# Transfers of the attention sums, their place in a written order, and a smaller piece for an accumulating DMA

## The chip, the cores and the metric

The kernel runs on one core of one Trainium2 chip. A core has five engines: TensorE (PE; its weight loads are listed as PEld), VectorE (DVE), ScalarE (ACT), GpSimd (POOL) and SyncE (SP), which here only issues DMAs. Sixteen DMA engines move the data. The metric is the device time of one execution in microseconds; the median of three runs before the change is 3682.39 us.

## The reference

A batch of 32 sequences of 256 tokens with 256 features goes through two layers. The first layer, cut to what matters here:

```
x  = x + attn(cond(x))                    # cond: modulated linear, attention over the 16 heads
                                          # of one token, modulated linear
                                          # attn: 16 heads of 16, normed queries and keys, gated
h  = adapter(x, cond_512)                 # per-sequence weights: x W_down relu W_up + x
x  = x + h-block:  h1 = h + self_attention(layer_norm(h))
                   moe(layer_norm(h1))    # 8 experts, top 2, capacity a quarter of the tokens
```

The second layer (a modulated linear map, an elementwise attention, a conditioned network, a butterfly FFN) follows. A softmax attention is computed for each head as exp(scores) times values, divided by the sum of the exp's; these divisors are the "sums" below.

## The kernel before, in words

The program has two phases. The first one runs, for each of the 32 sequences, everything up to the expert router (`sequence`); the second runs the experts and the second layer. Each phase's steps are written as Python generators. A step says `yield ENGINE, cost` ahead of the instructions that it issues, `yield None, t` for a time in which it only waits, `yield DMA, t` for a time on the shared transfer path, and takes and gives back buffers or turns (`Turns(n)`: n may be inside at a time). `side_by_side` reads these costs, keeps a clock for each engine, and always lets the step go on that can start first, where a step's `rank` breaks ties; the rank is the sequence's number plus the entry of its stage in the table `STAGES`. The result is one fixed order of instructions on every engine, made when the program is built. The costs are no times of the chip: they only decide the order. On the chip every engine runs its own list in order and waits at the head of it when an operand is not there. SP's DMAs and POOL's DMAs are such lists too. At most nine sequences are under way (`lanes`).

What the change touches, by name and line:

- `head_softmax_attention` (from L765): the attention over heads of a token. For sequences 3 to 31, `summed` adds two products of 128 x 2048 floats into one by a DMA with `accum_op=add` that POOL issues (L848, on buffers `hprod` of the ring `hp`, which has 5); then DVE halves the rest three times (L854, L856) and scales (L858). There are two such DMAs for each of these 29 sequences.
- `attention` (from L1033), run twice for each sequence. Scores (L1081), exp (L1090), answers (L1063), copied to `avT` (L1070). Of every 32 rows of `avT`, the first 16 hold answers and row 16 a sum. Behind the stage `tokens`: a DMA brings the sums into `den` as 128 x 32 (L1109); DVE takes reciprocals (L1118, into `den` or `sums`); a DMA stores them to `rden` in HBM (L1120); four DMAs move half of the answers up beside the others (L1124); a DMA reads `rden` back, each row repeated for 16 features, into `oT` (L1128); DVE multiplies (L1135).
- `residual_in`: loads `x` (L1188); POOL adds a bias row (L1190). `adapter_weights`: loads two rows to all partitions (L1172, L1174); POOL makes `wd` (L1177, L1178) and `wu` (L1181, L1182), which have two buffers each. TensorE uses them at L1306 and L1323.
- `layer_norm`: DVE's statistics (L366, L367), POOL's power (L261, L267, called `rstd`), DVE's scaling (L289, `xh`). The norms of queries take POOL's power at the same lines (called `n`), and DVE uses them at L918. The same POOL list holds L848, L1190, and these.

The DMAs of the first phase are issued by SP, except for L848 and one early load.

Of the kernel before, what the change touches and what calls it, by code (L numbers as in the profile page):

```python
# [14 lines left out]
F = mybir.dt.float32  # L15
I32 = mybir.dt.int32
AF = mybir.ActivationFunctionType
ALU = mybir.AluOpType
# [4 lines left out]
P = 128  # L23
S = 256
D = 256
H = 16
DH = 16
# [7 lines left out]
PE, DVE, ACT, POOL, SP = "PE", "DVE", "ACT", "POOL", "SP"  # L35
DMA = "DMA"
DVE2 = "DVE2"
POW = "POW"
# [61 lines left out]
def side_by_side(parts, lags):  # L100
# [84 lines left out]


STAGES = {
    "in": -0.5,
    "heads": 30.0,
    "answers of heads": 6.5,  # L190
    "sums of heads": -6.5,
    "out of heads": -25.0,
    "queries": 11.5,
    "queries by token": -7.5,
    "scores 1": -15.0,
    "tokens 1": 20.5,
    "out 1": 0.5,
    "x1": -12.0,
    "adapter": -13.0,
    "norm 1": -12.5,  # L200
    "queries 2": 26.0,
    "scores 2": -29.0,
    "tokens 2": 4.0,
    "out 2": -0.5,
    "norm 2": -5.5,
    "gates": -19.0,
    "values": 8.5,
    "norms of queries": -6.0,
    "answers": 8.0,
    "tokens": 8.0,  # L210
    "residual in": -4.5,
    "adapter's weights": 21.5,
    "bias": 24.5,
    "residual out": 16.0,
}


# [1 line left out]
def network(ctx: ExitStack, tc: tile.TileContext, a: dict, out: bass.AP):  # L219
    nc = tc.nc  # L220
    T = out.shape[0]
    B = T // S
# [8 lines left out]
    dpool = ctx.enter_context(tc.tile_pool(name="dpool", bufs=1, space=DRAM))  # L231
# [4 lines left out]
    rbuf = rrows[:T, :].rearrange("(b p t) d -> b p (t d)", p=P, t=2)  # L236
    gbuf = dpool.tile([2 * T, 1], F, name="gbuf")
    DS = 2 * H
    rden = dpool.tile([2, B, P, DS], F, name="rden")
    gtab = dpool.tile([B, 2 * HID + 2 * D], F, name="gtab")  # L240

    ident = cst.tile([P, P], F, name="ident")
# [92 lines left out]
    def back(r):  # L335
        return "back", rings[r][2]
# [22 lines left out]
    def layer_norm(sm, x2, name):  # L359

        yield DVE, lengths["moments"]
        st = sm.tile([P, 2, 6], F, name="st")
        mv = sm.tile([P, 2, 2], F, name="mv")
        rstd = sm.tile([P, 2], F, name="rstd")
        for t in range(2):
            nc.vector.bn_stats(st[:, t, :], x2[:, t, :])  # L366
            nc.vector.bn_aggr(mv[:, t, :], st[:, t, :])  # L367
        yield lengths["power"], 1.25
        rsqrt(rstd, mv[:, :, 1], 2, LN_EPS)
        xh = yield from get("sh", name)  # L370
        yield DVE, 0.75
        normalize(xh, x2, mv, rstd)
        return xh
# [364 lines left out]
    sums = {}  # L738
# [26 lines left out]
    def head_softmax_attention(kk, o0, b, exact):  # L765
# [78 lines left out]
        def summed(t, one, two):  # L844

            yield "stage", "sums of heads"
            yield POOL, 1.3
            nc.gpsimd.dma_start(one, two, accum_op=ALU.add)  # L848
            yield DMA, 7.0
            yield None, 2.0  # L850
            yield back("hp")
            for n in (4, 2):
                yield DVE2, 0.1 + 0.27 * n
                nc.vector.tensor_tensor(one[:, :n], one[:, :n], one[:, n : 2 * n], ALU.add)  # L854
            yield DVE2, 0.8
            nc.vector.tensor_tensor(o0[:, t, :], one[:, 0], one[:, 1], ALU.add)  # L856
            o = o0[:, t, :].rearrange("p (h d) -> p h d", h=H)
            nc.vector.tensor_tensor(o, o, rs[:, t].unsqueeze(2).to_broadcast([P, H, DH]), ALU.mult)  # L858
            yield back("hp")
# [173 lines left out]
    def attention(l, hT, b, exact, beside=None):  # L1033


        va = vaug[l]
        qT = yield from get("qk", "qT")
        kT = yield from get("kT", "kT", TS)
        vals = Part(values(l, hT))
        if l == 1:  # L1040
            yield vals
            yield from cosine_queries_and_keys(hT, qT, kT)
        else:
            yield from plain_queries_and_keys(hT, qT, kT)
            yield vals
        if beside is not None:
            yield "join", beside
        yield "join", vals
        yield back("sh")
        nm = None  # L1050
        if exact and l == 2:
            both = yield from get("hp", "both")
            nm = yield from row_maxima(qT, kT, both)
        yield "stage", f"scores {l}"

        avT = yield from get("avT", "avT")

        def answers(c, pt, av):
            yield "stage", "answers"
            yield PEC, 0.9  # L1060
            for kc in range(2):
                for i in range(4):
                    nc.tensor.matmul(  # L1063
                        av[32 * i : 32 * i + 32, c % 2, :], va[:, kc, HO * (4 * c + i) : HO * (4 * c + i) + 32], pt[:, i, kc, :],
                        start=(kc == 0), stop=(kc == 1),
                    )
            yield back("pt")
            if c % 2 == 1:
                yield ACT, 0.6
                nc.scalar.copy(avT[:, c - 1 : c + 1, :], av)  # L1070
                yield back("av")

        last = None
        for c in range(4):
            m, e = c // 2, c % 2
            sc = yield from get("sc", "sc")
            yield PER, 0.98
            for kc in range(2):
                for i in range(4):
                    r = slice(32 * i, 32 * i + 32)  # L1080
                    nc.tensor.matmul(  # L1081
                        sc[:, i, kc, :], kT[r, m, kc * P : (kc + 1) * P], qT[r, e, m, :], start=True,
                        stop=nm is None,
                    )
                    if nm is not None:
                        r = slice(32 * i, 32 * i + 1)
                        nc.tensor.matmul(sc[:, i, kc, :], ones[r, :], nm[r, c, :], start=False, stop=True)
            pt = yield from get("pt", "pt")
            yield EXP, 1.88
            nc.scalar.activation(pt, sc, AF.Exp, scale=1.0 / math.sqrt(DH))  # L1090
            yield back("sc")
            if last is not None:
                yield "join", last
            if c % 2 == 0:
                av = yield from get("av", "av")
            last = Part(answers(c, pt, av))
            yield last
        if nm is not None:
            yield back("hp")
        yield back("qk")  # L1100
        yield back("kT")
        yield "join", last
        yield "back", vaug_turn[l]
        yield "stage", f"tokens {l}"

        den = yield from get("den", "den")
        lanes_of = avT.rearrange("(i s d) c x -> i s d (c x)", i=4, s=2)
        yield SP, 0.6
        nc.sync.dma_start(  # L1109
            den[:, 0, :], lanes_of[:, 1, 0].rearrange("i (k x) -> i k x", x=DS)  # L1110
        )
        yield None, 2.8
        rd = den[:, 1, :]
        if l == 2 and not exact:
            rd = sums[b // NR][:, 1, 2 * (b % NR) : 2 * (b % NR) + 2, :].rearrange("p t h -> p (t h)")
        oT = yield from get("sh", "oT", TS)
        yield DVE, 0.37
        nc.vector.reciprocal(rd, den[:, 0, :])  # L1118
        yield SP, 1.0
        nc.sync.dma_start(rden[l - 1, b], rd)  # L1120
        for i in range(4):
            r = 32 * i + DH
            yield SP, 0.6
            nc.sync.dma_start(avT[r : r + DH, :2, :], avT[r - DH : r, 2:, :])  # L1124
        yield None, 0.4
        yield back("den")
        yield SP, 0.6
        nc.sync.dma_start(  # L1128
            oT.rearrange("p c s -> p (c s)"),
            rden[l - 1, b].rearrange("(g k) x -> g (k x)", g=8).unsqueeze(1).to_broadcast([8, DH, 2 * S]),  # L1130
        )
        yield DMA, 1.5
        yield None, 2.3
        yield DVE2, 0.75
        nc.vector.tensor_tensor(oT, avT[:, :2, :], oT, ALU.mult)  # L1135
        yield back("avT")
        return oT
# [28 lines left out]
    def adapter_weights(b, wd, wu):  # L1166
# [5 lines left out]
        nc.sync.dma_start(g1, gtab[b : b + 1, : 2 * HID].to_broadcast([P, 2 * HID]))  # L1172
        yield SP, 1.0
        nc.sync.dma_start(g2, gtab[b : b + 1, 2 * HID :].to_broadcast([P, 2 * D]))  # L1174
        yield None, 2.5
        yield POOL, 1.6
        nc.gpsimd.tensor_tensor(wd, wdn, g1[:, :HID].unsqueeze(1).to_broadcast([P, 2, HID]), ALU.mult)  # L1177
        nc.gpsimd.tensor_tensor(wd, wd, g1[:, HID:].unsqueeze(1).to_broadcast([P, 2, HID]), ALU.add)  # L1178
# [6 lines left out]
    def residual_in(b, x):  # L1185
        yield "stage", "residual in"
        yield SP, 1.0
        nc.sync.dma_start(x, a["x"][b * S : (b + 1) * S, :].rearrange("(t p) d -> p t d", p=P))  # L1188
        yield POOL, 1.3
        nc.gpsimd.tensor_tensor(x, x, rowA("bo1").unsqueeze(1).to_broadcast([P, 2, D]), ALU.add)  # L1190

# [14 lines left out]

    lanes = Turns(9)
    pair_turn = Turns(1)

    def sequence(b, exact):  # L1210

# [60 lines left out]
        x = yield from get("sh", "x")  # L1272
        res = Part(residual_in(b, x))
        yield res
        wd = sm.tile([P, 2, HID], F, name="wd", bufs=2)
        wu = sm.tile([P, D], F, name="wu", bufs=2)
        wts = Part(adapter_weights(b, wd, wu))
# [43 lines left out]
        for t in range(2):  # L1321
            r = slice(t * HID, (t + 1) * HID)
            nc.tensor.matmul(ps[t], act[r, :], wu[r, :], start=True, stop=True)  # L1323
        yield back("sh")
        yield DVE, 0.85
        for t in range(2):
            nc.vector.tensor_add(c2[:, t, :], ps[t], x1[:, t, :])
# [1204 lines left out]
```

## Time and profile before

| | us |
|---|---|
| three runs | 3684.66, 3678.87, 3682.39; median 3682.39 |
| the profiled execution | 3687.47 |
| its span, from the first to the last instruction | 3685.7 |
| TensorE busy | 3461.0 (94%) |
| VectorE busy | 2256.0 (61%) |
| GpSimd busy | 1914.8 (52%) |
| ScalarE busy | 1791.0 (49%) |
| mean granted TensorE clock | 0.976 |

Busy time is that of instructions; waiting at the head of a list and issuing DMAs from SP is not in it. A wait is put down to what came last by the profile. TensorE's matmuls overlap and their ends are modelled, so its busy share is an upper bound of work.

### The profile page before, as it was taken

The numbers are of one execution on the slowest core, as the hardware profiler recorded it, in microseconds if no ns is written. First come the engines' busy times: TensorE is split into PE (matmuls) and PEld (weight loads), VectorE is DVE, ScalarE is ACT, GpSimd is POOL, SyncE is SP. The second block draws the span as 40 slices with busy tenths as digits, with TensorE's granted clock in tenths as the row PEclk, the third lists the DMA queues.
The fourth block names the chain that finished last, engine by engine and source line by source line (L and its number), as shares of the span: only waits on it lengthen the run. The fifth ranks groups of instructions, "written<-read, shape, count | busy, mean of one in ns | idle before, by whom it ended". The sixth has DMA issues, their size and how long they took to land. (4 is left out here: it accounts for less than half of the span.)

```text
span 3685.7 us, 54807 instructions
## 1 busy us (share of the span) xinstructions
PE 3461.0 (94%) x21429; PEld 2525.1 (69%) x21429; DVE 2256.0 (61%) x3608; ACT 1791.0 (49%) x2761; POOL 1914.8 (52%) x1571
## 2 busy tenths in 40 slices
PE   6898999899999999959999999999979999999999
PEld 5565666566666665636666666666968888888888
DVE  7897889888888884566664531101355656555554
ACT  2786777777777777732222222222223343333433
POOL 2666655554455654335546565553044656565553
PEclk9999999999999999979999999999989999999999
DMA  1333444443444442143334343332341323232331
GB/s 65 74 84 92 100 91 96 97 95 92 95 97 94 96 97 68 52 144 86 79 96 100 91 92 55 58 67 46 126 143 55 114 92 97 95 107 92 117 95 43
DMA packets 179406, 329.51 MB, mean 89 GB/s; under 512 B 42465, under 2 KB 104097, under 8 KB 169154
## 3 DMA queue, kind: packets, MB, share of 16 engines
q0 software_dynamic: 56480, 161.59, 19.8%
q1 hardware_dynamic: 122514, 163.79, 14.1%
q8 instruction: 172, 2.82, 0.3%
q14 instruction: 96, 0.79, 0.1%
q10 hardware_dynamic: 144, 0.52, 0.0%
HBM read 204.03 MB, written 51.53 MB: 69 GB/s over the span
## 5 line engine op out<-in xcount | busy, mean ns | idle before, releaser
L1090 ACT ACTIVATE pt<-sc 128x2048 f32<-128x2048 f32 x256 | 480.8, 1878 | 113.8 <-PE sc L1081 104.7
L1702 ACT ACTIVATE hid<-bh,cols 128x512 f32<-128x512 f32 x254 | 173.8, 687 | 620.5 <-PE bh L1713 602.0
L1728 PE MATMUL by<-w,hid 128*128 128x256 f32 x2048 | 454.1, 380 | 2.5 <-DVE ysb L1734 2.5
L1713 PE MATMUL bh<-ehT,w 128*128 128x512 f32 x1024 | 451.1, 594 | 1.1 <-DVE ysb L1734 1.1
L1728 PEld LDWEIGHTS by<-w,hid 128*128 128x128 f32 x2048 | 387.9, 191 | 68.3 <-issue 15.3
L267 POOL TENSOR_TENSOR n<-n,negh 128x32 f32<-128x32 f32 x64 | 362.8, 5669 | 5.3
L1636 POOL DMA_INDIRECT rrows<-ysb,row x128 | 216.0, 1687 | 251.6 <-DMA rrows<-ysb,row 142.0
L1713 PEld LDWEIGHTS bh<-ehT,w 128*128 128x128 f32 x1024 | 194.8, 191 | 221.0 <-issue 214.9
L1734 DVE TENSOR_TENSOR ysb<-by,b 128x512 f32<-128x512 f32 x64 | 44.0, 688 | 471.4 <-PE by L1728 384.5
L1081 PE MATMUL sc<-qT,kT 32*128 32x256 f32 x4096 | 297.7, 405 | 22.3 <-ACT pt L1090 22.0
L1063 PE MATMUL av<-pt,vaug 128*32 128x256 f32 x4096 | 279.9, 392 | 8.0 <-ACT pt L1090 7.8
L1081 PEld LDWEIGHTS sc<-qT,kT 32*128 32x128 f32 x4096 | 187.4, 186 | 120.9 <-issue 52.9
L893 DVE TENSOR_TENSOR hprod<-hex,kk 128x2048 f32<-128x2048 f32 x116 | 264.8, 2305 | 0.0
L2359 PE MATMUL dh<-zT,w_eff 128*128 128x256 f32 x1024 | 235.3, 379 | 0.0
L1669 POOL DMA_INDIRECT xg<-h2buf,tok x128 | 148.8, 1163 | 161.4 <-issue 54.3
L2373 PE MATMUL do<-w_con,gT 128*128 128x256 f32 x1024 | 230.9, 379 | 0.0
L2373 PEld LDWEIGHTS do<-w_con,gT 128*128 128x128 f32 x1024 | 192.3, 190 | 24.9
L261 POOL TENSOR_SCALAR rstd<-mv 128x2 f32<-128x2 f32 x160 | 61.7, 386 | 281.3 <-DVE mv L367 271.2
L2359 PEld LDWEIGHTS dh<-zT,w_eff 128*128 128x128 f32 x1024 | 189.9, 190 | 23.6 <-DVE zT L2335 0.3
L1063 PEld LDWEIGHTS av<-pt,vaug 128*32 128x32 f32 x4096 | 108.1, 110 | 133.6 <-issue 64.3
L848 POOL DMA_DIRECT2D hprod<-hprod x58 | 53.3, 924 | 252.7 <-DVE hprod L893 208.7
L793 DVE TENSOR_TENSOR hprod<-kk 128x2048 f32<-128x2048 f32 (+1 forms) x96 | 162.6, 1694 | 12.3 <-ACT kk L1240 6.2
(620 smaller groups left out, 7267.9 us busy)
## 6 DMA issues: line engine op xcount, KB each, us to landing
hprod<-hprod POOLq DMA_DIRECT2D x58, 1024.0 KB
oT<-rden SPq DMA_DIRECT2D x64, 256.0 KB
w<-in_w SPq DMA_DIRECT2D x16, 1024.0 KB
x<-rrows SPq DMA_DIRECT2D x64, 256.0 KB
bfw<-in_upw SPq DMA_DIRECT2D x10, 1024.0 KB
bfw<-in_dnw SPq DMA_DIRECT2D x10, 1024.0 KB
xT<-in_xT SPq DMA_DIRECT2D x32, 256.0 KB
avT<-avT SPq DMA_DIRECT2D x256, 32.0 KB
```

Of the source, the lines that this page charges most:

```text
L267: nc.gpsimd.tensor_tensor(o, o, negh[:p].to_broadcast([p, n]), ALU.pow)
L793: nc.vector.tensor_tensor(pr, kk[:, :, :w].unsqueeze(2).to_broadcast([P, 2, n, w]), windows(kk, j0, n)[:, :, :, :w], ALU.mult)
L893: nc.vector.tensor_tensor(pr.rearrange("p j (h d) -> p j h d", d=DH), weights(t, j0, 8)[:, 0].unsqueeze(3).to_broadcast([P, 8, H, DH]), wi ...
L1063: nc.tensor.matmul(av[32 * i : 32 * i + 32, c % 2, :], va[:, kc, HO * (4 * c + i) : HO * (4 * c + i) + 32], pt[:, i, kc, :], start=(kc == ...
L1081: nc.tensor.matmul(sc[:, i, kc, :], kT[r, m, kc * P : (kc + 1) * P], qT[r, e, m, :], start=True, stop=nm is None,)
L1090: nc.scalar.activation(pt, sc, AF.Exp, scale=1.0 / math.sqrt(DH))
L1636: nc.gpsimd.indirect_dma_start(rrows[:, :], bass.IndirectOffsetOnAxis(ap=row[:, j0 + t : j0 + t + 1], axis=0), y[:, t, :], None, compute_o ...
L1702: nc.scalar.activation(o, ps, AF.Relu, bias=bcol)
L1713: nc.tensor.matmul(ps, w["w1"][:, c, f * P : (f + 1) * P], hT[c], start=(c == 0), stop=(c == 1))
L1728: nc.tensor.matmul(ps[:, t, :], hid[f // 4][:, f % 4, (t0 + t) * P : (t0 + t + 1) * P], w["w2"][:, f, :], start=(f == 0), stop=(f == 7),)
L2359: nc.tensor.matmul(ps[:, g, :], w_eff[:, c, f * P : (f + 1) * P], zT[:, c, :], start=(c == 0), stop=(c == 1))
L2373: nc.tensor.matmul(ps[:, t, :], gT[:, f, t * P : (t + 1) * P], w_con[:, f, :], start=(f == 0), stop=(f == 7))
```

## The change

The table `STAGES` gets other values for all 27 stages. In the accumulating DMA an argument, 512, caps the last dimension of a piece. The DMA of the sums into `den` becomes four, one for each group of 32 partitions. `rden` has twice as many rows; the reciprocals are stored twice, so that the read into `oT` has 16 groups of 8 in its outer dimensions where it had 8 groups of 16. Some costs that `side_by_side` reads are other numbers, with a new wait of 3.5 behind the load of `x`. A new turn, `adapter_turn`, lets two sequences at a time be between the taking of the adapter's weights and its last matmul.

```diff
--- before.py
+++ after.py
@@ -185,33 +185,33 @@
 
 
 STAGES = {
-    "in": -0.5,
-    "heads": 30.0,
-    "answers of heads": 6.5,
-    "sums of heads": -6.5,
-    "out of heads": -25.0,
-    "queries": 11.5,
-    "queries by token": -7.5,
-    "scores 1": -15.0,
-    "tokens 1": 20.5,
-    "out 1": 0.5,
-    "x1": -12.0,
-    "adapter": -13.0,
-    "norm 1": -12.5,
-    "queries 2": 26.0,
-    "scores 2": -29.0,
-    "tokens 2": 4.0,
-    "out 2": -0.5,
-    "norm 2": -5.5,
-    "gates": -19.0,
-    "values": 8.5,
-    "norms of queries": -6.0,
-    "answers": 8.0,
-    "tokens": 8.0,
-    "residual in": -4.5,
-    "adapter's weights": 21.5,
-    "bias": 24.5,
-    "residual out": 16.0,
+    "in": -3.0,
+    "heads": 25.5,
+    "answers of heads": 18.5,
+    "sums of heads": -24.5,
+    "out of heads": 20.5,
+    "queries": 17.5,
+    "queries by token": -14.5,
+    "scores 1": -25.0,
+    "tokens 1": -23.0,
+    "out 1": 25.5,
+    "x1": -29.5,
+    "adapter": -15.5,
+    "norm 1": -1.5,
+    "queries 2": 27.0,
+    "scores 2": -29.5,
+    "tokens 2": -4.0,
+    "out 2": 28.5,
+    "norm 2": -26.5,
+    "gates": -7.0,
+    "values": -3.5,
+    "norms of queries": -24.0,
+    "answers": 9.5,
+    "tokens": -29.5,
+    "residual in": -14.5,
+    "adapter's weights": 30.0,
+    "bias": 7.0,
+    "residual out": -30.0,
 }
 
 
@@ -236,7 +236,7 @@
     rbuf = rrows[:T, :].rearrange("(b p t) d -> b p (t d)", p=P, t=2)
     gbuf = dpool.tile([2 * T, 1], F, name="gbuf")
     DS = 2 * H
-    rden = dpool.tile([2, B, P, DS], F, name="rden")
+    rden = dpool.tile([2, B, 2 * P, DS], F, name="rden")
     gtab = dpool.tile([B, 2 * HID + 2 * D], F, name="gtab")
 
     ident = cst.tile([P, P], F, name="ident")
@@ -365,7 +365,7 @@
         for t in range(2):
             nc.vector.bn_stats(st[:, t, :], x2[:, t, :])
             nc.vector.bn_aggr(mv[:, t, :], st[:, t, :])
-        yield lengths["power"], 1.25
+        yield lengths["power"], 1.6 if lengths["power"] == POW else 1.25
         rsqrt(rstd, mv[:, :, 1], 2, LN_EPS)
         xh = yield from get("sh", name)
         yield DVE, 0.75
@@ -845,7 +845,7 @@
 
             yield "stage", "sums of heads"
             yield POOL, 1.3
-            nc.gpsimd.dma_start(one, two, accum_op=ALU.add)
+            nc.gpsimd.dma_start(one, two, accum_op=ALU.add, max_dma_last_dim=512)
             yield DMA, 7.0
             yield None, 2.0
             yield back("hp")
@@ -1105,32 +1105,35 @@
 
         den = yield from get("den", "den")
         lanes_of = avT.rearrange("(i s d) c x -> i s d (c x)", i=4, s=2)
-        yield SP, 0.6
-        nc.sync.dma_start(
-            den[:, 0, :], lanes_of[:, 1, 0].rearrange("i (k x) -> i k x", x=DS)
-        )
-        yield None, 2.8
+        for i in range(4):
+            yield SP, 0.58
+            nc.sync.dma_start(
+                den[32 * i : 32 * i + 32, 0, :], lanes_of[i : i + 1, 1, 0].rearrange("i (k x) -> i k x", x=DS)
+            )
+        yield None, 3.2
         rd = den[:, 1, :]
         if l == 2 and not exact:
             rd = sums[b // NR][:, 1, 2 * (b % NR) : 2 * (b % NR) + 2, :].rearrange("p t h -> p (t h)")
         oT = yield from get("sh", "oT", TS)
         yield DVE, 0.37
         nc.vector.reciprocal(rd, den[:, 0, :])
-        yield SP, 1.0
-        nc.sync.dma_start(rden[l - 1, b], rd)
+        into = rden[l - 1, b].rearrange("(g r k) x -> g r k x", g=8, r=2)
+        for r in range(2):
+            yield SP, 0.38
+            nc.sync.dma_start(into[:, r], rd)
         for i in range(4):
             r = 32 * i + DH
-            yield SP, 0.6
+            yield SP, 0.58
             nc.sync.dma_start(avT[r : r + DH, :2, :], avT[r - DH : r, 2:, :])
         yield None, 0.4
         yield back("den")
         yield SP, 0.6
         nc.sync.dma_start(
             oT.rearrange("p c s -> p (c s)"),
-            rden[l - 1, b].rearrange("(g k) x -> g (k x)", g=8).unsqueeze(1).to_broadcast([8, DH, 2 * S]),
+            rden[l - 1, b].rearrange("(g k) x -> g (k x)", g=16).unsqueeze(1).to_broadcast([16, DH // 2, 2 * S]),
         )
         yield DMA, 1.5
-        yield None, 2.3
+        yield None, 3.0
         yield DVE2, 0.75
         nc.vector.tensor_tensor(oT, avT[:, :2, :], oT, ALU.mult)
         yield back("avT")
@@ -1172,7 +1175,7 @@
         nc.sync.dma_start(g1, gtab[b : b + 1, : 2 * HID].to_broadcast([P, 2 * HID]))
         yield SP, 1.0
         nc.sync.dma_start(g2, gtab[b : b + 1, 2 * HID :].to_broadcast([P, 2 * D]))
-        yield None, 2.5
+        yield None, 3.5
         yield POOL, 1.6
         nc.gpsimd.tensor_tensor(wd, wdn, g1[:, :HID].unsqueeze(1).to_broadcast([P, 2, HID]), ALU.mult)
         nc.gpsimd.tensor_tensor(wd, wd, g1[:, HID:].unsqueeze(1).to_broadcast([P, 2, HID]), ALU.add)
@@ -1186,6 +1189,7 @@
         yield "stage", "residual in"
         yield SP, 1.0
         nc.sync.dma_start(x, a["x"][b * S : (b + 1) * S, :].rearrange("(t p) d -> p t d", p=P))
+        yield None, 3.5
         yield POOL, 1.3
         nc.gpsimd.tensor_tensor(x, x, rowA("bo1").unsqueeze(1).to_broadcast([P, 2, D]), ALU.add)
 
@@ -1206,6 +1210,7 @@
 
     lanes = Turns(9)
     pair_turn = Turns(1)
+    adapter_turn = Turns(2)
 
     def sequence(b, exact):
 
@@ -1272,6 +1277,7 @@
         x = yield from get("sh", "x")
         res = Part(residual_in(b, x))
         yield res
+        yield adapter_turn
         wd = sm.tile([P, 2, HID], F, name="wd", bufs=2)
         wu = sm.tile([P, D], F, name="wu", bufs=2)
         wts = Part(adapter_weights(b, wd, wu))
@@ -1322,6 +1328,7 @@
             r = slice(t * HID, (t + 1) * HID)
             nc.tensor.matmul(ps[t], act[r, :], wu[r, :], start=True, stop=True)
         yield back("sh")
+        yield "back", adapter_turn
         yield DVE, 0.85
         for t in range(2):
             nc.vector.tensor_add(c2[:, t, :], ps[t], x1[:, t, :])
```

## The prediction, made before the change was run

> **What bounds the kernel now.** I read the page's busy shares and its 40 slices first: they say in which stretch there is anything to win.
>
> ```profile
> PE 3461.0 (94%) x21429; PEld 2525.1 (69%) x21429; DVE 2256.0 (61%) x3608; ACT 1791.0 (49%) x2761; POOL 1914.8 (52%) x1571
> ...
> PE   6898999899999999959999999999979999999999
> ...
> DVE  7897889888888884566664531101355656555554
> ```
>
> TensorE is nearly full everywhere, and VectorE only in the first 16 slices: that is the first phase. So I cut the span at the phase's edges with the table of stretches (after the span: PE, PEld, DVE, ACT, POOL busy, each with its count, then granted clock, DMA share, GB/s):
>
> ```profile
> 0.00:184.00 184.00, 142.91 (x860) 105.09 (x860) 149.30 (x173) 87.02 (x149) 89.53 (x46) 0.93 0.26 70
> 184.00:1390.00 1206.00, 1127.86 (x10021) 740.86 (x10013) 1034.61 (x1458) 923.17 (x1359) 683.87 (x459) 0.98 0.40 94
> 1390.00:1564.00 174.00, 162.02 (x1538) 106.07 (x1535) 88.90 (x179) 125.74 (x165) 72.47 (x60) 0.98 0.23 60
> 1564.00:1612.00 48.00, 29.96 (x253) 21.19 (x250) 20.53 (x45) 19.67 (x23) 4.45 (x7) 0.82 0.15 47
> 1612.00:3685.70 2073.70, 1998.26 (x8773) 1551.91 (x8773) 962.69 (x1755) 635.37 (x1068) 1064.53 (x1000) 0.98 0.33 92
> ```
>
> The first phase ends near 1612 us; behind it nothing is edited. TensorE's idle time in the phase is 41.1 + 78.1 + 12.0 + 18.0 = 149 us. As no matmul is added or removed, that is all that can be won (the modelled busy time may hide a little more). In the middle PE is 94% busy, DVE 86%, POOL 57%.
>
> Then the waits of the phase (0 to 1612 us), engine by engine: total, times, longest.
>
> ```profile
> DVE xh L289 <- POOL rstd L267: 44.2, 33, 8.7
> DVE sums L1118 <- DMA den<-avT: 42.4, 14, 6.7
> ...
> DVE oT L1135 <- DMA oT<-rden: 27.6, 11, 7.6
> DVE qk L918 <- POOL n L267: 23.8, 19, 5.7
> ...
> POOL x L1190 <- DMA x<-in_x: 112.6, 16, 12.3
> ...
> PE mm L297 <- DVE xh L289: 28.3, 12, 7.0
> ```
>
> Two kinds of stall start from a DMA that lands later than the written order supposes: DVE at the sums' transfers (42.4 + 27.6 = 70 us), and POOL at the residual (112.6 us). The second one does its harm through what is queued behind it. The timeline at 523 us shows it:
>
> ```profile
> 523.27 0.87 POOL L848 DMA_DIRECT2D hprod<-hprod  x1 [4.79 <-DVE hprod L893]
> 534.93 1.51 POOL L1190 TENSOR_TENSOR x<-x,rowsA 128x512 f32<-128x512 f32 x1 [10.79 <-DMA x<-in_x]
> ...
> 538.98 0.19 POOL L261 TENSOR_SCALAR rstd<-mv 128x2 f32<-128x2 f32 x1
> ...
> 540.00 0.73 DVE L289 TENSOR_SCALAR xh<-c,mv,rstd 128x256 f32<-128x256 f32 x2 [4.68 <-POOL rstd L267]
> ```
>
> The statistics for `rstd` were ready at 532.6; POOL stood 10.8 us at the head of its queue for `x`, then DVE stood 4.7 us and PE 2.0 us.
>
> Why does `x` take so long? From the trace's semaphore steps I took issue to landing for every SP DMA of the phase, apart by whether a packet of an accumulating DMA ran meanwhile (medians, alone / beside): `den` 2.00 / 6.11 us, `avT` 1.95 / 4.59, `rden` 1.41 / about 5, `oT` 3.92 / 8.87, `x` 3.67 / 7.31. (A long landing meets such a DMA more easily, so the gap is overstated.) The accumulating DMA is 128 packets of 8192 B, eight on each of 16 engines, 642 ns each: 5.1 us of engine time, landing 8.1 us after issue. An SP packet waits its turn behind them. The `den` semaphore gets 5 steps (4 engines and one up front), `oT` 9 (8 engines), the others 16.
>
> **The change part by part.**
>
> *The written order* (STAGES, and waits of 3.2, 3.0, 3.5 and 3.5 us where there were 2.8, 2.3, 2.5 and none; 1.6 for the power). No instruction is added. The residual's add is now placed 3.5 us after its issue where 0 stood, so the 112.6 us wait at POOL should mostly fill with other POOL work. What it frees is the `rstd` and `n` behind it: DVE waits 44.2 + 23.8 = 68 us for these. All 27 priorities change too, which moves every step of the phase and every DMA that they issue past each other on SP, POOL, ACT, DVE and PE; the trace of before can't show the new order, and I bound it by PE's idle: at best some 90 of the 149 us go, at worst the waits grow by about a third (+50 us).
>
> *`den` in four DMAs.* Three issues more by 0.58 us: the last starts 1.75 us later. 64 x 1.75 = 112 us more on SP. By the row, `den` on 4 engines lands alone in 2.00 us, and `avT` on 16 engines in 1.95: alone the split gains nothing and costs 1.75 us. The Trainium skill speaks against it as well ("DMA: Bandwidth & Descriptors", section "Rules for kernel authors": two transfers to disjoint halves of the partitions end up serialised on the same engines, so make one). By rule alone it is +1.75 us per chain. But the row beside an accumulate says 6.11: 32 packets of `den` queue on each of 4 engines, and with 2 on each of 16 it should be near `avT`'s 4.6. So +1.7 alone, about 0 beside.
>
> *`rden` twice, `oT` on 16 engines.* One issue more of 0.32 us (20 us of SP in all), and 8 packets of 84 ns on an engine in place of 16: -0.7 us. The chain from the last `avT` copy to the product was 2.00 + 0.34 (reciprocal) + 0.3 + 2.35 (four `avT` issues) + 0.3 + 3.92 = 9.2 us alone and becomes 10.3. Nothing but SP's queue stands behind the extra issues: SP issues about 400 us of DMAs in the phase and gets 132 more, 33% of 1612. In the middle other sequences cover the 1.1 us; at the end, where the last sequence stands alone (1564 to 1612), they add about 2 us, or nearly 4 if two chains are bare.
>
> *The accumulating DMA in pieces of 512.* If these are elements, 2048 B each. An accumulating packet of 1024 B (the scatter L1636, into HBM) takes 102 ns and one of 8192 B 642: a line through both gives 179 ns for 2048 B, 32 on an engine, 5.7 us for 5.1. That +0.6 us lies beside other work: DVE waited for this DMA once, 6.0 us. The turn that an SP packet waits shrinks from 642 to 179 ns, so the surcharge beside an accumulate (+4.1 `den`, +4.9 `oT`, +3.6 `x`) falls to about 1 us each. The skill says otherwise ("DMA: Bandwidth & Descriptors", "SWDGE vs HWDGE vs iDMA"): GpSimd's DMAs are put into packets of up to 4096 B, and an engine changes queues only between packets; that would be 0.36 us a turn, a surcharge of 2 us. In the trace the gathers are packed so (rows of 1024 B show as 4096 B), but the accumulating scatter is not, it shows 16384 packets of 1024 B, so I take 179 ns.
> POOL's issue (L848) took 924 ns for 128 pieces. No row has more pieces. Ends: no change, or in proportion, 3.7 us. I take 1.5, near the lower end, as 924 ns for one piece on a partition is likely mostly fixed: +0.6 x 58 = 35 us of POOL. The written order allots 1.3 us to the issue before and after, so nearly all of it lies in a gap that is kept for it; without that cover it delays an `n` or `rstd`.
>
> *Turns of the adapter's weights.* From the residual's issue to the last adapter matmul of its sequence is 20 to 64 us, median 47; sequences come every 46 us, so two turns rarely bind, and both buffers made the same limit before. Nothing; if it binds, a sequence waits while eight others run.
>
> **Sum.** Outside the ramp, DVE makes PE wait 78 us in the phase (28.3 for `xh`, the rest for `qk`, `oT`, `x1`, `gate`). Of DVE's own 294 us of listed waits, 70 are these DMAs and 68 POOL, together 47%. I take that share of PE's 78 us as removed: -37; the end +2, SP's and POOL's longer issues +2: -33. The profiled execution took 3687.5 us (span 3685.7): 3654.5. The median of the three runs, 3682.4, is 5.1 lower: 3649.
>
> **The rivals.**
>
> *PE is full anyway.* Where DVE no longer waits, PE next waits for ACT (`sc` for `pt`, 22.0 us) or has no work; PE's middle is 94% busy at a clock of 0.98. For: the 112.6 us at POOL reach PE as a few tens only. Then -7 to +7: 3682.
>
> *Slower: the pieces are cut too fine, and POOL pays.* The call says 512 without a unit; if it counts bytes, the change doesn't do what its name says. Then there are 2048 pieces, 128 on an engine by 64 ns (same line), 8.2 us, landing near 11 instead of 8.1, and POOL writes 16 times as many. In the middle POOL has 522 us free for 52 such issues: 10 us each until it is the bound. It hurts sooner: beyond the allotted 1.3 us, if half of the 58 issues delay an `n` or `rstd`, each microsecond costs 29 us of DVE idle and, by PE's idle to DVE's in the middle (78 to 171), 13 us. The gain of 33 is eaten at +2.5 us, an issue of 3.8. At 6 us: 4.7 x 13 - 33 = +28, 3710; in proportion, 14.8 us, POOL is full and the time near 3900. Against: what a plain issue costs beyond its pieces is not known, and most of 924 ns may be fixed.
>
> *The new order is itself worse.* Priorities of 27 stages set anew may leave PE waiting for ACT or for buffers: +10 to +50, 3712 in the middle.
>
> **How the numbers follow.** About 0.2% (7 us) is what a measurement can tell. Forecast (8 to 90 us gained) 0.67; no change 0.11; pieces 0.13; order 0.09. So faster 0.67, same 0.11, slower 0.22. Predicted 3649. Low end 3597 (85 us gained, over half of PE's idle); high end 3712, the middle of both slow cases; the forecast's own range is 3597 to 3672.
>
> **What would show it.** Right: the wait of POOL at L1190 under 40 us, DVE's at L1118 and L1135 together under 35; `den` and `oT` landing beside an accumulate within 2 us of alone; PE idle in the phase down to about 115 us; the phase ending near 1579. Packets on the software queue tell the unit: 56480 + 58 x 384 = 78752 for elements, 167840 for bytes. L848's mean tells POOL's price: under 2 us right, over 3.8 the slow rival. Wrong: these waits gone and the phase as long, with PE waiting for ACT or DVE for PE (first rival), or DVE waiting more for `rstd` and `n`.

## The result, and the profile after

The changed kernel is slower: 3730.78 us median (3728.37 to 3734.96, 4 runs) against 3683.52 us of the kernel before beside it (3678.87 to 3684.91, 4 runs); ratio 1.0132, 95% interval 1.0118 to 1.0147. That is +47 us where -33 was forecast. The profiled execution took 3732.95 us, its span 3731.2.

The page's busy shares and slices of the kernel after, with the row of the DMA engines:

```profile
PE 3474.3 (93%) x21429; PEld 2533.9 (68%) x21429; DVE 2231.5 (60%) x3608; ACT 1793.7 (48%) x2761; POOL 1973.2 (53%) x1571
...
PE   6898989998899899969999999999998999999999
...
DVE  6887787788788786456664541001345655565554
...
DMA  1465555655555555123324343332341323222321
```

The same row of the kernel before:

```profile
DMA  1333444443444442143334343332341323232331
```

Slices 2 to 16 carry 4 to 6 tenths, mostly 5, where they carried 3 to 4. That is the one large difference between the pages. The table of stretches of the kernel after, cut at the same places as before's and at its own end of the phase (us, then busy us of PE, PEld, DVE, ACT, POOL, then granted clock, DMA share, GB/s):

```profile
0.00:184.00 184.00, 139.59 (x824) 102.62 (x826) 148.06 (x171) 83.90 (x143) 95.19 (x44) 0.93 0.32 61
184.00:1390.00 1206.00, 1098.33 (x9612) 719.98 (x9608) 969.95 (x1399) 888.06 (x1304) 710.28 (x445) 0.96 0.58 92
1390.00:1612.00 222.00, 209.61 (x2000) 138.76 (x1997) 135.97 (x248) 168.50 (x226) 97.97 (x75) 1.00 0.34 67
1612.00:1657.00 45.00, 27.19 (x229) 19.18 (x228) 15.92 (x37) 16.91 (x21) 6.68 (x9) 0.78 0.18 56
1657.00:3731.20 2074.20, 1999.61 (x8774) 1553.39 (x8774) 961.58 (x1755) 636.28 (x1069) 1063.03 (x1000) 0.98 0.33 92
```

The second phase takes 2074.2 us, as before (2073.7). The whole loss lies in the first, which ends at 1657 where it ended near 1612. In the middle stretch the DMA engines are busy 58% of the time and were 40%, while the rate is 92 GB/s and was 94: more engine time for the same bytes. TensorE does 1098 us of work in these 1206 us, before 1128.

The waits of the phase (0 to 1657 us) in the kernel after:

```profile
DVE sums L1119 <- DMA den<-avT: 81.4, 20, 10.5
POOL x L1194 <- DMA x<-in_x: 54.8, 11, 18.7
DVE oT L1138 <- DMA oT<-rden: 30.4, 11, 7.5
PE sc L1081 <- ACT pt L1090: 28.1, 27, 4.4
DVE hprod L854 <- DMA hprod<-hprod: 23.2, 10, 5.9
DVE qk L918 <- POOL n L267: 22.6, 20, 2.7
DVE xh L289 <- POOL rstd L267: 20.4, 21, 2.6
DVE den L1119 <- DMA den<-avT: 16.3, 5, 8.1
PE av L1063 <- ACT pt L1090: 15.3, 9, 6.2
PE mm L309 <- ACT xT L1228: 11.1, 6, 4.7
```

POOL's wait for `x` halved (112.6 to 54.8) and DVE's for `rstd` too (44.2 to 20.4): these waits move the way the written order meant. But DVE now waits 98 us for the sums in its two rows (44), and 23 us at L854 for the accumulating DMA, for which it waited once before (6.0). The queue, issue and landing of that DMA, first before, then after (queue: packets, MB, share; the line of its issue: busy, mean ns, idle before; last, KB and median us from issue to landing):

```profile
q0 software_dynamic: 56480, 161.59, 19.8%
...
L848 POOL DMA_DIRECT2D hprod<-hprod x58 | 53.3, 924 | 252.7 <-DVE hprod L893 208.7 <-DVE sums L1118 14.3 <-DVE gate L1163 9.9
```

```profile
q0 software_dynamic: 167840, 161.59, 26.0%
...
L848 POOL DMA_DIRECT2D hprod<-hprod x58 | 124.2, 2156 | 222.0 <-DVE hprod L893 166.4
...
hprod<-hprod POOLq DMA_DIRECT2D x58, 1024.0 KB, 12.6
```

167840 packets is to the packet the number that the prediction gave for bytes: the pieces are of 512 bytes, 128 floats, 2048 to a DMA. In the trace such a packet takes 74 ns (median), and a DMA 9.6 us on each of the 16 engines where whole rows took 5.35. The landing went from 8.1 to 12.6 us.

### The profile page after: what moved, and what is told of

The parts are those of the page before. It is cut to its first block, busy times and chain, and to the rows that moved or that the text cites. A ratio compares the mean times of both kernels' runs of the same rounds, so it can differ in the third digit from the quotient of the medians.

```text
span 3731.2 us, 55238 instructions
## 1 busy us (share of the span) xinstructions
PE 3474.3 (93%) x21429; PEld 2533.9 (68%) x21429; DVE 2231.5 (60%) x3608; ACT 1793.7 (48%) x2761; POOL 1973.2 (53%) x1571
## 3 DMA queue, kind: packets, MB, share of 16 engines
q0 software_dynamic: 167840, 161.59, 26.0%
## 5 line engine op out<-in xcount | busy, mean ns | idle before, releaser
L893 DVE TENSOR_TENSOR hprod<-hex,kk 128x2048 f32<-128x2048 f32 x116 | 272.6, 2372 | 0.0
L848 POOL DMA_DIRECT2D hprod<-hprod x58 | 124.2, 2156 | 222.0 <-DVE hprod L893 166.4
L261 POOL TENSOR_SCALAR n<-n 128x32 f32<-128x32 f32 x64 | 43.5, 680 | 240.3 <-DVE n L939 214.8
## 6 DMA issues: line engine op xcount, KB each, us to landing
hprod<-hprod POOLq DMA_DIRECT2D x58, 1024.0 KB, 12.6
```

What stands on the lines that cost most here:

```text
L893: nc.vector.tensor_tensor(pr.rearrange("p j (h d) -> p j h d", d=DH), weights(t, j0, 8)[:, 0].unsqueeze(3).to_broadcast([P, 8, H, DH]), wi ...
```

## The experiments

Every time stands beside runs of the kernel before on the same chip, whose median moved between 3683 and 3688 us; the ratio is the measure. Where a difference between two rows changes when each is set against its own runs of before, both figures are given. "Phase end" is the last copy of the router's logits in the trace, "PE idle" TensorE's idle time up to it.

| kernel | us | ratio to before (95%) | phase end | PE idle |
|---|---|---|---|---|
| before | 3683.5 | 1 | 1609 | 147 |
| after | 3730.8 | 1.0132 (1.0118 to 1.0147) | 1657 | 182 |
| e1 after, whole rows | 3681.0 | 0.9978 (0.9970 to 0.9986) | 1603 | 146 |
| e2 before, pieces of 512 | 3769.7 | 1.0219 (1.0199 to 1.0239) | 1691 | 201 |
| e3 order alone | 3645.8 | 0.9887 (0.9866 to 0.9907) | 1565 | 118 |
| e4 before, split | 3724.7 | 1.0104 (1.0081 to 1.0127) | 1642 | 172 |
| f1 order, den in four | 3664.3 | 0.9934 (0.9913 to 0.9956) | 1589 | 140 |
| f2 order, rden twice | 3644.5 | 0.9880 (0.9856 to 0.9903) | 1564 | 117 |
| f3 order, pieces of 2048 | 3638.1 | 0.9863 (0.9842 to 0.9884) | 1567 | 116 |
| p1 before, POOL kept busy | 3694.6 | 1.0025 (1.0016 to 1.0033) | 1619 | 151 |
| q1 order, SP kept busy | 3648.4 | 0.9908 (0.9888 to 0.9927) | 1573 | 124 |
| f4 before, pieces of 2048 | 3694.4 | 1.0035 (1.0022 to 1.0047) | 1621 | 153 |
| h1 after, order told of late sums | 3740.0 | 1.0167 (1.0145 to 1.0188) | 1659 | 179 |
| g2 order, old priorities | 3686.4 | 1.0009 (1.0002 to 1.0016) | 1604 | 146 |
| g3 before, new priorities | 3711.6 | 1.0067 (1.0045 to 1.0088) | 1635 | 156 |
| l1 before, DMA load | 3852.7 | 1.0455 (1.0436 to 1.0475) | 1773 | 273 |
| b1 order, 2048, rden twice | 3641.9 | 0.9883 (0.9863 to 0.9903) | 1567 | 120 |

### The change in three parts: e1, e2, e3, e4

e1 is the kernel after with whole rows:

```diff
-            nc.gpsimd.dma_start(one, two, accum_op=ALU.add, max_dma_last_dim=512)
+            nc.gpsimd.dma_start(one, two, accum_op=ALU.add)
```

> The changed kernel with the cap of 512 taken from the accumulating DMA (whole rows of 8192 B again), all else as changed. Theory P (the pieces: the accumulating DMA lands 12.6 us after issue where it took 8.1, and fills the DMA engines for 9.6 us where it took 5.3): 3675 to 3695, L848 lands near 8 us again. Theory O (the new order is worse by itself): 3720 to 3735. Theory S (the sums' transfers in more DMAs hold SP and land late): 3720 to 3735.

e2 makes the opposite edit in the kernel before, and no other.

> The kernel before with the cap of 512 on the accumulating DMA alone; every list of instructions keeps its order. Theory P: 3715 to 3735. Theories O and S: 3680 to 3690, with the landing of L848 at 12 to 13 us and hidden.

e3 keeps the whole new order (priorities, costs, waits, turn) and has the transfers of before:

```diff
-            nc.sync.dma_start(
-                den[32 * i : 32 * i + 32, 0, :], lanes_of[i : i + 1, 1, 0].rearrange("i (k x) -> i k x", x=DS)
-            )
+            if i == 3:
+                nc.sync.dma_start(
+                    den[:, 0, :], lanes_of[:, 1, 0].rearrange("i (k x) -> i k x", x=DS)
+                )
...
-            nc.sync.dma_start(into[:, r], rd)
+            if r == 1:
+                nc.sync.dma_start(rden[l - 1, b], rd)
```

> The changed order of the first phase (priorities, costs, waits and adapter turns as changed) with the transfers of before: whole rows in the accumulating DMA, one DMA for den, one store to rden, 8 groups in the read into oT. Theory O: 3715 to 3735. Theory P: 3650 to 3690. Theory S: 3650 to 3690, and lower than the changed kernel with whole rows (e1) by over 15 us.

e4 is the kernel before, in its order, with den in four DMAs, `rden` twice and `oT` in 16 groups.

> The order of before with the changed transfers of the sums alone: den in four DMAs, rden stored twice, oT read in 16 groups; whole rows in the accumulating DMA. Theory S: 3705 to 3735, with over 80 us of DVE waiting at the reciprocals of den. Theories O and P: 3678 to 3692.

The order alone gains 42 us (3645.8 against 3688.2 beside it), near the forecast's 37. The split then costs 35 (e1 minus e3; e4 says the same on the old order, +36), and the small pieces 50 on top by the medians (after minus e1), 55 beside each one's own runs of before; on the old order they cost 82 (e2, more than was expected of it). -42 + 35 + 55 is the +47 that was measured, as it must be, since each is a step from one kernel to the next. Small pieces without the split, in the new order, were not run. So the forecast was not one wrong guess but two costs taken for almost nothing.

### Why the order gains: g2, g3

g2 is e3 with the table `STAGES` of before; g3 is the kernel before with the new table and the turn of the adapter's weights, and none of the new waits.

```diff
 STAGES = {
-    "in": -3.0,
-    "heads": 25.5,
...
+    "in": -0.5,
+    "heads": 30.0,
...
```

> The changed order's waits, costs and turn (3.5 us behind the load of x, 3.5 for the adapter's rows, 3.0 for oT, 3.2 for den, 1.6 for the power, two turns of the adapter's weights), but the table of priorities of the kernel before; whole rows, no split. The whole new order gained 42 us (3645.8). Recorded forecast (the gain comes from the steps that now wait for measured landings): 3640 to 3660, with POOL's wait for x near 60 us or less. Theory priorities (the table carries the gain): 3675 to 3695.

> The kernel before with the changed table of 27 priorities and the turn of the adapter's weights, and none of the changed waits and costs; whole rows, no split. The new order as a whole gained 42 us (3645.8), its waits with the old table nothing (3686.4). Theory priorities (the table carries the gain, the waits nothing): 3640 to 3658. Theory both (the table was found for these waits and gives its gain only with them): 3670 to 3700, or slower, with POOL waiting over 100 us for x.

Neither does it alone: the waits with the old table gain nothing (3686.4, ratio 1.0009), the new table without the waits loses 25 us, and both together gain 42. The waits of g2 in its phase (0 to 1604 us):

```profile
PE sc L1081 <- ACT pt L1090: 40.3, 36, 4.3
POOL x L1195 <- DMA x<-in_x: 34.5, 10, 10.0
DVE qk L918 <- POOL n L267: 31.2, 28, 3.6
DVE xh L289 <- POOL rstd L267: 23.9, 31, 1.3
PE av L1063 <- ACT pt L1090: 18.7, 18, 2.4
DVE oT L1139 <- DMA oT<-rden: 17.7, 7, 6.9
DVE sums L1120 <- DMA den<-avT: 11.5, 4, 6.2
```

The waits at DMAs that the forecast wanted gone are small: POOL for `x` 34.5 (it was 112.6), DVE for `den` and `oT` 29 (70). Both are within the limits that the prediction set for being right. DVE's waits behind POOL, which were to go with them, fell less, from 68 to 55. Yet the phase is as long as before. The sums of TensorE's own waits in the phase say where it went: for DVE 100 us before and 68 in g2; for ACT 37 before and 66 in g2. What TensorE no longer waits for at DVE it waits for at the exponentials. Their rows before:

```profile
PE sc L1081 <- ACT pt L1090: 22.0, 24, 4.4
PE av L1063 <- ACT pt L1090: 7.8, 9, 2.3
```

With the new table too (e3) the rows read:

```profile
PE sc L1081 <- ACT pt L1090: 14.9, 20, 1.5
PE av L1063 <- ACT pt L1090: 10.0, 8, 2.0
PE mm L297 <- DVE xh L289: 6.4, 2, 3.7
```

In all 77 for DVE and 32 for ACT. e3 has more of the waits at these DMAs than g2 (64.5 us for `x`, 59 for `den` and `oT`) and is 41 us shorter. Only DVE's wait behind POOL is lower, 35 us. So removing the waits at the DMAs does not bring the gain by itself; the table and the waits bring it together. Which of the 27 entries do it, and by which wait, stays open.

### The split: f1, f2, q1

f1 is the new order with only den in four (e1 with before's `rden` and `oT`); f2 has only `rden` twice and `oT` in 16 groups.

> The changed order with whole rows in the accumulating DMA, and of the split only the sums' DMA into den in four; rden stored once, oT read in 8 groups. Without any split this order took 3645.8 us, with the whole split 3681.0: +35. Theory SP (each added issue holds SP's queue and so delays all that SP issues behind it; the split's two parts share the 35 us by their SP time, 64 x 2.6 = 166 us here and 64 x 1.0 = 64 us in the other part): +25, 3671. Theory chain (only the chain's own length counts; den in four makes it 0.8 us longer and the rden part nothing): the whole +35, 3681. Theory rden (the loss comes from rden's two stores of 0.65 us each): no loss here, 3646 to 3651.

> The changed order with whole rows in the accumulating DMA, and of the split only rden stored twice with oT read in 16 groups; den by one DMA. Theory SP: +10, 3656. Theory chain: no loss, 3642 to 3650. Theory rden: +30, 3676. The oT read should land in some 5.5 us beside other work as in the kernel with the whole split, where it took 7.3 without.

Den in four costs 18.5 us by the medians (20 beside own runs of before), `rden` twice nothing (-1 to 0), though it holds SP for 1.31 us where one store took 0.32. Together they cost 35, more than the sum; why was not settled. q1 asks whether the three added issues do it, by issues for nobody behind a single den:

```diff
             if i == 3:
                 nc.sync.dma_start(
                     den[:, 0, :], lanes_of[:, 1, 0].rearrange("i (k x) -> i k x", x=DS)
                 )
+                for j in range(3):
+                    nc.sync.dma_start(aside[l - 1, b, j], ones[32 * j : 32 * j + 32, :DS])
```

> The changed order with whole rows and one den DMA (3645.8 us), with three more DMAs of 4 KB that nobody waits for, from a constant into HBM, issued on SP right behind each den; den itself keeps its place. With den in four the same order took 3664.3, +18.5. Theory SP's queue (the three added issues of some 0.6 to 0.8 us delay what SP issues behind them): +12 to +20, 3658 to 3666. Theory den (the sums themselves arrive later, since their last quarter is issued 2.7 us after the first): -3 to +6, 3643 to 3652.

They cost 2.6 us by the medians and 7 beside own runs of before, and the intervals overlap: SP's queue bears the smaller part, which may still be over a third. The rest is left to the arrival of the sums themselves; waits of f1, then of q1, each in its phase:

```profile
DVE sums L1119 <- DMA den<-avT: 57.9, 16, 10.5
DVE oT L1138 <- DMA oT<-rden: 29.2, 8, 7.0
...
DVE den L1119 <- DMA den<-avT: 11.5, 4, 6.0
DVE oT L1138 <- DMA den<-avT: 11.2, 3, 4.5
```

```profile
DVE oT L1141 <- DMA oT<-rden: 35.8, 11, 7.3
DVE sums L1122 <- DMA den<-avT: 33.9, 9, 8.8
```

DVE waits 81 us for den in four, 34 for one den. Over the 64 chains of f1 the four issues took 3.3 us (mean) from the start of the first to the end of the last, against 0.6 for one in e3, and the last landing came only 0.3 us sooner after that (2.6 against 3.0). From the first issue to the last landing that is 6.0 us where one den took 3.6: +2.4 us for each chain.

### The pieces: p1, f3, f4, h1, l1

POOL's price first. p1 puts an operation for nobody behind each accumulating issue, in the order of before:

```diff
-            nc.gpsimd.dma_start(one, two, accum_op=ALU.add)
+            nc.gpsimd.dma_start(one, two, accum_op=ALU.add); nc.gpsimd.tensor_tensor(spare, spare, negh.to_broadcast([P, 4]), ALU.pow)
```

> The kernel before, with 58 small operations on POOL (power of 128 x 4, by the rows near 1.2 us) added right behind the accumulating DMAs' issues, in the same order; this lays POOL's extra price for small pieces (2.16 - 0.92 = 1.23 us) alone on the old order, where the small pieces themselves cost 82 us. Its output is unchanged. Theory POOL (POOL's price is what hurts; the recorded rival's 13 us for each us of price would give +16 and did not suffice, so then its rate must be 65): +60 to +85, 3745 to 3770. Theory landing (what hurts is that the sum lands 13 us after its issue where the order allots 10.3, and the engines' 4.3 us more for each DMA; POOL's price is small): +5 to +20, 3692 to 3708.

The operation came out longer than meant, and still cost only 8 to 9 us:

```profile
L848 POOL TENSOR_TENSOR spare<-spare,negh 128x4 f32<-128x4 f32 x58 | 105.5, 1820 | 0.0
```

1.82 us on POOL is more than the 1.23 us that the small pieces add there. POOL's price is about a ninth of the 82 us.

f3 and f4 cap the pieces at 2048 bytes, 512 elements, on the new order and on the old one (`max_dma_last_dim=2048`).

> The changed order without the split, the accumulating DMA in pieces of 2048 bytes (512 elements, what the name of the change says), 512 pieces where 128 are whole rows. Recorded forecast: 179 ns a packet, 32 on an engine, 5.7 us, landing about 8.7, POOL's issue 1.5 us at most, and SP's DMAs beside it land 2 to 3 us sooner: the same as without or a little faster, 3636 to 3648. Theory of the packets' fixed cost (a line through 8192 B at 642 ns and 512 B at 75 ns, as now measured, gives 189 ns, 6.0 us a DMA; POOL's issue on the line through 128 pieces at 0.92 and 2048 at 2.16 us gives 1.17; SP's DMAs land no sooner): landing 8.8, 0 to +8, 3646 to 3654.

> The kernel before, with pieces of 2048 bytes in the accumulating DMA and nothing else; 512 bytes cost it 82 us. Recorded forecast (SP's DMAs beside it land sooner): -5 to -20, 3668 to 3683. Theory landing (a term that the order's 10.3 us covers costs little; it should land near 9): 0 to +8, 3688 to 3696. Theory pieces in proportion (512 pieces where 128 and 2048 are; a fifth of the 82): +16, 3704. On the changed order the same step gave 3638.1 against 3645.8.

These are the pieces that the forecast reckoned with: 188 ns a packet (179 forecast), 6.3 us a DMA (5.7), POOL's issue 1.35 us (1.5), landing 9.0. But SP's DMAs beside them came hardly sooner: in f4 `den` 6.8, `avT` 5.0, `oT` 8.3, `x` 6.4 us, medians, where whole rows gave 6.1, 4.6, 8.9 and 7.3. The time is +11 us on the old order; on the new one it is 6 to 8 us less than e3, with intervals that overlap; 3638 lies in the recorded forecast, but not for its reason, that SP's DMAs land 2 to 3 us sooner.

h1 is the kernel after whose order is told of the late sums:

```diff
-            yield POOL, 1.3
+            yield POOL, 2.2
             nc.gpsimd.dma_start(one, two, accum_op=ALU.add, max_dma_last_dim=512)
-            yield DMA, 7.0
+            yield DMA, 11.5
```

> The kernel after, with its 512-byte pieces and the split, where the written order is told what was measured: 2.2 us for POOL's issue in place of 1.3 and 11.5 us of transfer in place of 7.0. With whole rows the kernel after took 3681.0, with small pieces 3730.8. Theory late landing (the loss of 50 us comes from DVE's halvings being placed before the sum has landed): two thirds of it go, 3690 to 3705. Theory load (the sixteen engines carry 9.6 us a DMA where they carried 5.35, and that delays all other DMAs, wherever the steps stand): at most a fifth goes, 3720 to 3735. All steps of the phase can move, so +-15 either way is chance of the order.

DVE's wait for `hprod` at L854 fell from 23 to 5 us, its waits for den from 98 to 66, and the phase is as long (1659 against 1657); the time, 3740, is above what either theory gave. Placing the steps later does not bring the time back; as all steps move, this alone would be weak. l1 tests the load itself, with sums that land as before:

```diff
-            nc.gpsimd.dma_start(one, two, accum_op=ALU.add)
+            nc.gpsimd.dma_start(one, two, accum_op=ALU.add); nc.gpsimd.dma_start(aside[2 * b + t], rowsA.unsqueeze(1).to_broadcast([P, 3, N_ROWS_A]))
```

> The kernel before, with a second DMA on POOL's queue behind each of the 58 accumulating ones: 384 packets of 4096 B from a constant into HBM that nobody reads, by the row of such packets (159 ns) some 4 us on each of 16 engines, about what 512-byte pieces added (4.3 us). The sum itself lands as before, about 8.1 us after its issue; POOL pays one more issue of about 1 us, which by the run with POOL kept busy (1.8 us, +9) is worth +5. Theory load (the engines' added time delays SP's DMAs and through them the phase): +40 to +80, 3723 to 3763. Theory landing (the late sum itself is what costs): +5 to +20, 3688 to 3703.

+166 us, twice what small pieces cost and twice what was expected at most. The added packets took 159 ns (median), 4.1 us on each engine for each DMA, and the sum landed in 8.75 us (8.1). What became late are SP's DMAs beside it: `den` 11.5 us (6.1), `oT` 12.2 (8.9), `x` 13.6 (7.3). The waits of l1's phase:

```profile
POOL x L1190 <- DMA x<-in_x: 185.6, 17, 18.7
DVE sums L1118 <- DMA den<-avT: 115.1, 16, 14.6
...
DVE oT L1135 <- DMA oT<-rden: 50.5, 13, 7.3
```

So time on the engines beside SP's small DMAs is by itself enough to cost more than was lost. But l1 is no copy of the small pieces: it lacks their cut, writes to HBM, and makes SP's DMAs later than they do (in e2 `den` 7.0, `oT` 8.3, `x` 8.4 us). In e2 DVE also waits for the late sum, at the halvings and where a buffer of `hprod` is used again; in all 45 us, before 6:

```profile
DVE hprod L854 <- DMA hprod<-hprod: 23.6, 10, 5.9
DVE hprod L793 <- DMA hprod<-hprod: 21.4, 4, 10.5
```

Its waits for `den` and `oT` grew by 18 us and those at POOL by 13. How the 82 us divide between the late sum and the load stays open.

What an SP DMA waits for beside an accumulating one can be read from the packets. Taken were accumulating DMAs during which the queue moved nothing else, and of each the first SP DMA that was issued between 0.7 us before its first packet and 2.5 us before its last one, with no earlier SP DMA still under way. Alone, the first packet of such an SP DMA starts 0.8 to 1.3 us after its issue. Beside whole rows (before and e3, 22 cases) it starts 3.0 us later than that (median), beside 2048 bytes (f4 and f3, 18 cases) 3.3, and beside 512 bytes (e2, after and h1, 17 cases) 3.3. In this time an engine began 4 of its 8, 19 of its 32 and 57 of its 128 accumulating packets. So the added wait is about the same for all three sizes; what sets it stays open. Since small pieces keep the engines longer, more SP DMAs meet them: of the phase's 480 for `x` and for the sums' chains, 183 did before, 191 in f4 and 219 in e2.

### The best of them: b1

b1 is f2 with pieces of 2048 bytes.

> The changed order with the two parts that cost nothing there: pieces of 2048 bytes (3638.1 without the split) and rden stored twice with oT on 16 engines (3644.5 with whole rows), den in one DMA. Sum of parts against the order alone (3645.8): -7.7 - 1.3, 3637. Theory SP and engines add up as the split's two parts did (18.5 and -1 apart, 35 together): 3645 to 3660.

3641.9 us, no better than its parts. e3, f2, f3 and b1 cannot be told apart by their intervals; all beat both kernels, by 1.1 to 1.4% against before. The order is all that is worth keeping of the change.

## Why the prediction was wrong, point by point

- *TensorE's idle time as all that can be won.* The best runs end with 116 to 120 us idle, where "down to about 115" was named for right. But it was not all: e3's phase is 45 us shorter with the same matmuls, 29 of them idle time and 16 busy time (1463 to 1447). The sum priced only waits. The trace's record of the granted clock shows TensorE at half clock for 99.8 us of the phase before (19 spells), 139.5 us after (23), 185.0 in e2 (30), 74.2 in e3 (11). In the kernel after busy time went from 1463 to 1475 us: 12 of the 48 us lost there are slower matmuls, not waits.
- *The written order, -37.* The size was right (-42), by luck, since the step was not: "47% of PE's 78 us" supposes that a wait removed at DVE is time won at TensorE. g2 took 78 us from POOL's wait for `x` and 41 from DVE's for the sums and gained nothing, as the first rival said ("where DVE no longer waits, PE next waits for ACT"). And e3, which gains, keeps 64.5 and 59 us of them, over the limits of 40 and 35 that were to show the forecast right.
- *Den in four, "about 0 beside" and "in the middle other sequences cover".* This step failed. Beside an accumulating DMA of whole rows each of the four landed 5.39 us after its own issue (f1, median) and one den 5.36 (e3); 16 engines brought no relief. From the first issue to the last landing the four took 8.1 us there and one 5.8 (means), alone 4.0 and 2.1. The +2.4 us a chain were not covered: den in four cost 18.5 to 20 us in f1, and 35 with the `rden` part. The Trainium skill ("DMA: Bandwidth & Descriptors", "Rules for kernel authors") advised one transfer; I had that row, and put the neighbour's landing against it.
- *`rden` twice, +20 us on SP.* Mis-sized, without effect: one store of half the engines took 0.655 us to issue, so SP got 64 us more, not 20; `oT` alone landed 0.6 us sooner (3.9 to 3.3). Two slips of the working change nothing: the chain's 10.3 us leaves out the second store's 0.32, and 8 to 90 us gained are 3592 to 3674, not 3597 to 3672.
- *The pieces, "+0.6 us lies beside other work".* This step failed too, and cost most. The unit was taken wrongly: it is bytes, the slow rival's case, so the DMA took 4.3 us more of each engine and landed 4.5 us later, which cost 50 to 55 us on the new order and 82 on the old one. The rival estimated 8.2 us of engine time and a landing near 11; they were 9.6 and 12.6. But its price was put on POOL, deciding from 3.8 us an issue; POOL took 2.16, under that point, and by p1 POOL's time bears about a ninth. Its own working would have given a gain.
- *"The turn that an SP packet waits shrinks from 642 to 179 ns."* This step fails for elements too (f4). An SP DMA waited not one packet of the trace but about 3 us, 3.0 beside packets of 642 ns, 3.3 beside 188 and 3.3 beside 74. The skill has another turn on the same page, in a section that I did not weigh ("Queues, rings and completion order"): an engine takes its queues in turn by packets of typically 9 to 17 and at most 64 descriptors. If a packet of the trace is a descriptor of the page, which no run here shows, that rule does not come out of the counts either: a turn of 9 or more would hold all 8 whole rows of an engine, and an SP DMA issued just ahead of them (0.3 to 0.7 us before the first) began when 3 to 7 of the 8 were begun (before and e3).
- *The cases were kept apart.* Each rival changed one term and left the others at the forecast. The costs of the split and of the pieces, both outside their terms, came together; that took the time beyond the range's high end of 3712.
- *The adapter's turn, "nothing".* It was not tried alone.

## What to carry to other kernels

Price a DMA by its time on the engines and by which others are in flight beside it; the issuing engine's time can be the smallest part. When a forecast counts waits removed at one engine, look for what the bounding engine waits for next, and try the waits apart from the order. Check the unit of a size argument by its packet count before reckoning with it.

## What the runs showed of the hardware

- Accumulating packets inside SBUF took 642 ns for 8192 bytes, 188 for 2048 and 74 for 512: about 36 ns each and 74 ns for 1000 bytes more, one line through all three. POOL's issue took 0.92, 1.35 and 2.16 us for 128, 512 and 2048 of them, far less than in proportion.
- The first packet of an SP DMA started 0.8 to 1.3 us after its issue alone, and 3.0, 3.3 and 3.3 us later than that beside accumulating packets of 8192, 2048 and 512 bytes. Cutting these smaller did not let it in sooner.
- Stalls of a few us seem to cost TensorE twice: its spells at half clock, each a multiple of 3.41 us long but where the phase's end cuts one, grew with its idle time (74 us at 118 idle in e3, 185 at 201 in e2). The skill ("TensorE: Matmul & The Clock Gate", "What's actually happening") has a window of 3413 ns, and that agrees.
